# Longer transfers in the drain of a one-hot attention layer, and its last four blocks searched in wider segments

## The chip, the cores and the metric

The kernel runs on one core of a Trainium2 chip. The core has five engines, each with its own instruction queue: PE (matrix multiply; PEld is its weight load), DVE (vector), ACT (scalar functions), POOL (GpSimd) and SP (synchronisation; here it only issues transfers). Sixteen DMA engines move data between main memory and the on-chip memory. The metric is the device time of one execution in microseconds, as a median of several executions.

## The reference

`x` is 4096 x 512, `adj` is 4096 x 4096 (64 MB), `W` is 512 x 2048 (four heads), `a` is 4 x 1024 x 1, all in float32.

```python
ht = (h @ W).reshape(N, N_HEADS, N_HIDDEN).transpose(1, 0, 2)
src = jnp.einsum('hnd,hd->hn', ht, a_src)
dst = jnp.einsum('hnd,hd->hn', ht, a_dst)
e = jax.nn.leaky_relu(src[:, :, None] + dst[:, None, :], SLOPE) + adj_mat[None]
att = jax.nn.softmax(e, axis=-1)
h_prime = jnp.einsum('hij,hjd->hid', att, ht)
return h_prime.mean(axis=0)
...
x = _layernorm(x + _L0_gnn_ref(x, adj, L0_gnn_W, L0_gnn_a), axis=-1)
```

The nonzero entries of `adj` are random numbers up to 1e9 and are added to scores that are tiny beside them. So the softmax of a row is 1 at the largest entry of that row of `adj` and 0 elsewhere, as long as the largest leads the second by more than the scores can differ. Then the layer is: for each row find the column j of the largest entry, fetch `x[j]`, multiply it by the mean of the four heads' weights, add the row's own `x`, and normalise the row.

## The kernel before, in words

`leading_rows` does exactly that for all rows, and also proves on the chip that each row's largest entry leads by enough; a second function, `general`, does the full softmax and runs only if the proof fails for a row, which it does not on this data. The proof needs the two largest entries of each row, a bound from `W` and `a` (`head_norms`) and the largest norm of a row of `x` (`row_norm`, `bound`, `test`, `count`, `report`).

The 4096 rows are split into `NB` = 32 blocks of 128 rows, one row to a partition (row p * 32 + ib is partition p of block ib). For block `ib`:

- `load_adj` (L122, SP's queue) brings 128 rows of 16 KB of `adj`, 2 MB: whole for blocks 0 to 27, in halves for 28 to 30, in quarters for 31.
- `segment_maxima` (L169, DVE) takes the maximum of each segment of 16 columns (blocks 0 to 17, `E_EARLY`) or 32 columns (18 to 31, `E`): 256 or 128 maxima for a row.
- `find_segment` (L176, L178, DVE) finds the largest maxima of a row and the index of the first. Its index goes to POOL.
- `fetch_segment` (L185, L191, L198, POOL) turns the index into a row number (with `first`) and fetches that one segment of each row again from main memory with an indirect DMA into the tile `lead`; `start` is the segment's first column (with `width`).
- `find_column` (L208, L214, DVE; L216, L202, POOL) finds the column inside the segment and gathers the 128 rows `x[j]` into `y`. For block 31 `find_column_in_row` (L222) searches the whole row of 4096 on DVE instead, so that its gather waits for no segment.
- `turn` (PE transposes L229, ACT copy L231), `products` (PE, L244), `residual` (adds the row's own `x`, L237), `stats` (ACT), `rstd` (POOL) and `finish` (ACT, L277) end the block. The result overwrites the row's own `x` in the tile `hold` (32 x 512 numbers in each partition), and `store` (L329, SP's queue) writes it out.

Every engine runs its instructions in the order in which the program issues them. The loop over t = 0 to 31 runs the steps of different blocks in each turn: block t's maxima, block t - 2's column, block t - 3's products, block t - 6's end. `AHEAD` = 5 is how many blocks the loads run ahead.

**The drain.** `Q` = 4, `LATE` = 28, `BEHIND` = 24. `x` of blocks 24 to 27 is loaded last of all, after `adj` of block 31, at t = 31 (L441, two transfers of two blocks). Until it is there the products of 24 to 27 are kept in a spare buffer (`put_by`, L257), and `add_x` (L261) adds the `x`: on POOL for 24, 25 and 26, on DVE for 27. Stores of blocks 0 to 23 are issued only after the loop, behind every load on SP's queue: two of four blocks, then eight of two blocks (L482 to L485). After the loop POOL's order is: `add_x(24)` (L486), the column and the gather of block 30 (L487), the segment of block 31 (L488), `add_x(25)` (L489), the gather of block 31 (L490), `add_x(26)` (L491). DVE's order there is: the column of 30 (L214), the search of 31's row (L222), and later what ends blocks 28 to 31. The last stores (L540 to L542) go in this order: 28, 29, 24 with 25, 26 with 27, 30, 31.

Semaphores are placed by a framework: a transfer on SP's queue takes the next of eight completion semaphores in turn, and is not issued before the transfer eight places earlier has landed. Each of the 16 DMA engines raises the semaphore when its share has landed, and only all sixteen count as landed.

Of the kernel before, what the change touches and what calls it, by code (L numbers as in the profile page):

```python
# [9 lines left out]
F32 = mybir.dt.float32  # L10
U32 = mybir.dt.uint32
I32 = mybir.dt.int32
AF = mybir.ActivationFunctionType
OP = mybir.AluOpType
# [6 lines left out]
P = 128  # L21
C = 512
E = 32
E_EARLY = 16
EARLY = 18


@with_exitstack
# [40 lines left out]
def leading_rows(ctx, tc, x, adj, W, a, out, ident, v, n_bad, any_bad):  # L69
# [8 lines left out]
    nc = tc.nc  # L78
    N, D = x.shape
    H = a.shape[0]  # L80
    KB, NB, S = D // P, N // P, N // E
    S_EARLY = N // E_EARLY
    AHEAD = 5
    Q = 4
    PIECES = 4
    LATE = NB - Q
    BEHIND = LATE - Q

    once = ctx.enter_context(tc.tile_pool(name="once", bufs=1))
    adj_pool = ctx.enter_context(tc.tile_pool(name="adj_pool", bufs=AHEAD + 1))  # L90
    y_pool = ctx.enter_context(tc.tile_pool(name="y_pool", bufs=4))
    lead_pool = ctx.enter_context(tc.tile_pool(name="lead_pool", bufs=2 * Q + 1))
    small = ctx.enter_context(tc.tile_pool(name="small", bufs=5))
    rows = ctx.enter_context(tc.tile_pool(name="rows", bufs=2))
    psum = ctx.enter_context(tc.tile_pool(name="psum", bufs=4, space=bass.MemoryType.PSUM))

    adj_rows = adj.rearrange("(p nb) m -> nb p m", nb=NB)
    adj_segs = adj.rearrange("n (s e) -> (n s) e", e=E)
    adj_segs_early = adj.rearrange("n (s e) -> (n s) e", e=E_EARLY)
    x_rows = x.rearrange("(p nb) d -> p nb d", nb=NB)  # L100
    out_rows = out.rearrange("(p nb) d -> p nb d", nb=NB)
    w_blocks = W.rearrange("(kb p) (h d) -> p kb h d", p=P, h=H)
# [11 lines left out]
    def pieces(ib):  # L114
        return PIECES if ib == NB - 1 else 2 if ib >= LATE else 1

    def load_adj(ib):
        if 0 <= ib < NB:
            t = adj_t[ib] = adj_pool.tile([P, N], F32, name="adj_t")
            n = pieces(ib)  # L120
            for k in range(n):
                nc.sync.dma_start(t[:, ts(k, N // n)], adj_rows[ib][:, ts(k, N // n)])  # L122

    def load_x(lo, n):
        nc.sync.dma_start(hold[:, ds(lo, n), :], x_rows[:, ds(lo, n), :])
# [13 lines left out]

    make_identity(nc, ident)  # L140
    first = once.tile([P, NB], U32, name="first")
    nc.gpsimd.iota(first[:, :EARLY], pattern=[[S_EARLY, EARLY]], base=0, channel_multiplier=NB * S_EARLY)
    nc.gpsimd.iota(first[:, EARLY:], pattern=[[S, NB - EARLY]], base=EARLY * S, channel_multiplier=NB * S)
    ones = once.tile([P, P], F32, name="ones")
    nc.gpsimd.memset(ones, 1.0)
    width = once.tile([P, 2], U32, name="width")
    nc.gpsimd.iota(width, pattern=[[E_EARLY - E, 2]], base=E, channel_multiplier=0)
    power = once.tile([P, 3], F32, name="power")
    nc.gpsimd.memset(power, -0.5)
    eps = once.tile([P, 1], F32, name="eps")  # L150
# [6 lines left out]
    sd = once.tile([P, NB], F32, name="sd")  # L157
    lead_by = once.tile([P, 1], F32, name="lead_by")

    seg_of, at_of, lead_of, y_t, yt_of, o_ps = {}, {}, {}, {}, {}, {}  # L160

    def segment_maxima(ib, lo, hi):

        e = E_EARLY if ib < EARLY else E
        if lo == 0:
            seg_of[ib] = small.tile([P, N // e], F32, name=f"seg{e}", bufs=2)
        n = max(pieces(ib), 2)
        for k in range(lo * n // PIECES, hi * n // PIECES):
            nc.vector.tensor_reduce(  # L169
                seg_of[ib][:, ts(k, N // e // n)],  # L170
                adj_t[ib][:, ts(k, N // n)].rearrange("p (s e) -> p s e", e=e), axis=AX.X, op=OP.max,
            )
# [9 lines left out]
    def fetch_segment(ib):  # L182
        at = at_of.pop(ib)
        row = small.tile([P, 1], U32, name="row")
        nc.gpsimd.tensor_tensor(row, at[:, 0:1], first[:, ib : ib + 1], op=OP.add)  # L185
        early = ib < EARLY
        if early:
            lead = lead_pool.tile([P, E_EARLY], F32, name="lead_early", bufs=8)
        else:
            lead = lead_pool.tile([P, E], F32, name="lead")  # L190
        nc.gpsimd.indirect_dma_start(  # L191
            out=lead, out_offset=None, in_=adj_segs_early if early else adj_segs,
            in_offset=bass.IndirectOffsetOnAxis(ap=row[:, :1], axis=0),
        )
        lead_of[ib] = lead
        if ib < NB - 1:
            start = at_of[ib] = small.tile([P, 1], U32, name="start")
            nc.gpsimd.tensor_tensor(start, at[:, 0:1], width[:, int(early) : int(early) + 1], op=OP.mult)  # L198

    def gather_rows(ib, col):  # L200
        y = y_t[ib] = y_pool.tile([P, D], F32, name="y")
# [126 lines left out]
    def store(queue, lo, n):  # L328
        queue.dma_start(out_rows[:, ds(lo, n), :], hold[:, ds(lo, n), :])  # L329
# [93 lines left out]
    for t in range(NB):  # L423
        if t == NB // 2:
            tc.mark_branch_hint_location("general", engines=HINTED)
        if t in x_at:
            load_x(*x_at[t])
        if t + AHEAD == NB - 1:
            load_x(LATE, Q)
        load_adj(t + AHEAD)  # L430
        middle = 1 if t == NB - 1 else 2
        segment_maxima(t, 0, middle)
        if t >= COLUMN:
            find_column(t - COLUMN)
        segment_maxima(t, middle, PIECES)
        pair = FINISH <= t < BEHIND + FINISH and t % 2 == 0
        if pair:
            rstd(slice(t - FINISH, t - FINISH + 2))
        if t == NB - 1:
            for ib in (BEHIND, BEHIND + 2):  # L440
                load_x(ib, 2)  # L441
        find_segment(t)
        if t < 2:
            mean_of_heads(t)
        elif t == 2:
            mean_of_heads(2)
            mean_of_heads(3)
        if t == 0:
            turn_a()
        turned = [(*vectors[0], turn_w(*vectors.pop(0))) for _ in range(vectors_at.get(t, 0))]  # L450
        if t == 16:
            head_norms()
        ib = t - PROJECT
        if t == NB - 1:
            for late in range(LATE, NB):
                row_norm(late)
        if t == NB - 2:
            residual(LATE)
            residual(LATE + 1)
        if ib >= 0:  # L460
            turn(ib)
            if ib > BEHIND:
                products(ib - 1, KB - 1, KB)
            if ib < BEHIND:
                residual(ib)
        for some in turned:
            head_vector(*some)
        if ib >= 0:
            products(ib, 0, KB if ib < BEHIND else KB - 1)
        if t >= BEHIND + STATS:  # L470
            put_by(t - STATS)
        elif t >= STATS:
            stats(t - STATS)
            row_norm(t - STATS)
        if pair:
            finish(t - FINISH)
            finish(t - FINISH + 1)
# [1 line left out]
    for ib in range(BEHIND, LATE):  # L479
        row_norm(ib)  # L480
    nc.scalar.activation(xx, xx, AF.Sqrt)
    for ib in range(0, 2 * Q, Q):  # L482
        store(nc.sync, ib, Q)
    for ib in range(2 * Q, BEHIND, 2):
        store(nc.sync, ib, 2)  # L485
    add_x(nc.gpsimd, BEHIND)  # L486
    find_column(NB - 2)  # L487
    fetch_segment(NB - 1)  # L488
    add_x(nc.gpsimd, BEHIND + 1)  # L489
    find_column_in_row(NB - 1)  # L490
# [46 lines left out]
    moments(NB - 1)  # L537
    factor(NB - 1, shift=True)
    finish_in_halves(NB - 1)
    for ib, n in ((NB - 4, 1), (NB - 3, 1), (BEHIND, 2), (BEHIND + 2, 2), (NB - 2, 1)):  # L540
        store(nc.sync, ib, n)
    store(nc.sync, NB - 1, 1)  # L542

# [152 lines left out]
```

## Time and profile before

| What | us |
|---|---|
| median of three runs (235.43, 235.53, 236.70) | 235.53 |
| the profiled execution, its own time | 235.65 |
| its span, first to last instruction | 234.1 |
| around the span | 1.55 |
| DVE busy | 191.6 |
| PE busy | 197.5 |
| POOL busy | 100.3 |
| ACT busy | 111.6 |
| last quarter of `adj` of block 31 starts to be searched | 207.51 |
| gather of block 31 issued by POOL | 215.40 |
| first transpose of block 31 on PE | 222.62 |
| store of block 31 issued | 229.70 |

In the tables of the profile, L169 is line 169 of the kernel before. A row of the timeline has start, duration (both us), engine, line, operation, tile written and tiles read with their shapes, the number of instructions, and in brackets how long the engine was idle before and what ended that. A row of the windows has a stretch of time, its length, and for each engine the busy us in it; then the granted PE clock as a share, the mean busy share of the 16 DMA engines, and GB/s moved. In a row of waits stand the us waited in total, how often, and the longest.

Beside the tables the trace holds single DMA packets, with size and time, and the moment at which each of the 16 engines raised a transfer's semaphore. Where a size or a landing is given below without a table, it is from there.

### The profile page before, as it was taken

The numbers are of one execution on the slowest core, as the hardware profiler recorded it, in microseconds if no ns is written. First come the engines' busy times: TensorE is split into PE (matmuls) and PEld (weight loads), VectorE is DVE, ScalarE is ACT, GpSimd is POOL, SyncE is SP. The second block draws the span as 40 slices with busy tenths as digits, with TensorE's granted clock in tenths as the row PEclk, the third lists the DMA queues.
The fourth block names the chain that finished last, engine by engine and source line by source line (L and its number), as shares of the span: only waits on it lengthen the run. The fifth ranks groups of instructions, "written<-read, shape, count | busy, mean of one in ns | idle before, by whom it ended". The sixth has DMA issues, their size and how long they took to land.

```text
span 234.1 us, 2486 instructions
## 1 busy us (share of the span) xinstructions
PE 197.5 (84%) x683; PEld 101.6 (43%) x683; DVE 191.6 (82%) x300; ACT 111.6 (48%) x267; POOL 100.3 (43%) x212
## 2 busy tenths in 40 slices
PE   0198959999999699999999599859899967999980
PEld 0034525765656356555544144324333423344360
DVE  0566885589929999999789986999999999989871
ACT  2003012155665447475768264645564654187561
POOL 2022232415524464646443642646465464557400
PEclk9999778999999999999999979999999999999997
DMA  6999999999999999999999999999999999999994
GB/s 243 432 428 417 445 419 434 418 444 420 433 422 427 430 424 433 426 419 431 434 427 427 429 433 424 419 436 419 435 428 417 425 427 421 413 426 419 416 386 179
DMA packets 12977, 97.06 MB, mean 415 GB/s; under 512 B 2072, under 2 KB 2584, under 8 KB 7200
## 3 DMA queue, kind: packets, MB, share of 16 engines
q1 hardware_dynamic: 9360, 88.08, 89.0%
q0 software_dynamic: 3584, 8.77, 9.5%
q8 instruction: 6, 0.10, 0.2%
q14 instruction: 11, 0.09, 0.1%
q10 hardware_dynamic: 16, 0.02, 0.0%
HBM read 88.47 MB, written 8.39 MB: 414 GB/s over the span
## 4 chain that ended last, share of the span: by engine, by line
DMA 48%; POOL 19%; issue 17%; DVE 11%; PE 2%; ACT 0%; POOLq 0%; DVEq 0%; ACTq 0%; SPq 0%
DMA adj_t<-in_adj_dram 41%; DVE seg L169 8%; POOL y L202 6%; POOL lead L191 5%; DMA y<-in_x_dram,col 3%; DMA lead<-in_adj_dram,row 2%; POOL sd L272 2%; PE o L286 2%; DMA a_rows<-in_L_gnn_a_dram 1%; DVE col L222 1%; POOL row L185 1%; POOL start L198 1%; POOL col L216 1%; POOL lead_early L191 1%; DVE at L178 1%
## 5 line engine op out<-in xcount | busy, mean ns | idle before, releaser
L169 DVE TENSOR_REDUCE seg<-adj_t 128x128 f32<-128x2048 f32 (+2 forms) x66 | 145.4, 2207 | 29.0 <-DMA adj_t<-in_adj_dram 29.0
L244 PE MATMUL o<-w_sum,yt 128*128 128x512 f32 x248 | 116.0, 609 | 0.7 <-ACT yt L231 0.7
L244 PEld LDWEIGHTS o<-w_sum,yt 128*128 128x128 f32 x248 | 44.8, 193 | 53.9 <-issue 42.4
L231 ACT COPY yt<-tp 128x512 f32<-128x512 f32 x32 | 18.8, 587 | 45.8 <-PE tp L229 45.7
L202 POOL DMA_INDIRECT y<-in_x_dram,col x32 | 30.8, 961 | 16.5 <-POOL col L216 15.4
L334 PE MATMUL o<-hold,ident 128*128 128x512 f32 x32 | 20.9, 815 | 14.6 <-DMA hold<-in_L_gnn_W_dram 14.6
L229 PE MATMUL tp<-ident,y 128*128 128x128 f32 x128 | 19.7, 276 | 13.7 <-DMA y<-in_x_dram,col 13.7
L237 PE MATMUL o<-hold,ident 128*128 128x512 f32 x52 | 26.8, 600 | 0.0
L229 PEld LDWEIGHTS tp<-ident,y 128*128 128x128 f32 x128 | 14.4, 141 | 26.8 <-issue 25.5
L185 POOL TENSOR_TENSOR row<-at,first 128x1 uint32<-128x1 uint32 x32 | 6.0, 188 | 43.7 <-DVE at L178 43.3
L352 ACT COPY wt<-tp 128x512 f32<-128x512 f32 x16 | 9.2, 586 | 31.5 <-PE tp L350 31.5
L191 POOL DMA_INDIRECT lead_early<-in_adj_dram,row x18 | 18.1, 1008 | 8.9 <-POOL row L185 8.9
L216 POOL TENSOR_TENSOR col<-start,within 128x1 uint32<-128x1 uint32 x31 | 5.8, 188 | 36.0 <-DVE within L214 36.0
L251 ACT ACTIVATE sq<-hold 128x512 f32<-128x512 f32 x32 | 19.8, 619 | 0.0
L358 PEld LDWEIGHTS pv<-at_d,wt 128*128 128x128 f32 x128 | 16.3, 191 | 6.8 <-ACT wt L352 3.7
L334 PEld LDWEIGHTS o<-hold,ident 128*128 128x128 f32 x32 | 8.1, 265 | 25.1 <-issue 20.2
L335 ACT ACTIVATE w_sum<-o 128x512 f32<-128x512 f32 x4 | 2.4, 598 | 33.0 <-PE o L334 33.0
L277 ACT ACTIVATE hold<-o,nm,sd 128x512 f32<-128x512 f32 x24 | 17.2, 769 | 0.0
L191 POOL DMA_INDIRECT lead<-in_adj_dram,row x14 | 14.0, 1003 | 7.0 <-POOL row L185 7.0
L268 ACT ACTIVATE sq<-o,nm 128x512 f32<-128x512 f32 x24 | 16.5, 687 | 0.8
L358 PE MATMUL pv<-at_d,wt 128*128 128x2 f32 x128 | 15.3, 244 | 0.6 <-ACT wt L352 0.6
L266 ACT ACTIVATE sq<-o 128x512 f32<-128x512 f32 x24 | 14.6, 609 | 0.0
(91 smaller groups left out, 150.8 us busy)
## 6 DMA issues: line engine op xcount, KB each, us to landing
adj_t<-in_adj_dram SPq DMA_DIRECT2D x28, 2048.0 KB, 31.7
adj_t<-in_adj_dram SPq DMA_DIRECT2D x6, 1024.0 KB, 28.0
out_dram<-hold SPq DMA_DIRECT2D x10, 512.0 KB, 14.3
hold<-in_L_gnn_W_dram SPq DMA_DIRECT2D x4, 1024.0 KB, 18.8
hold<-in_x_dram SPq DMA_DIRECT2D x2, 2048.0 KB, 36.5
hold<-in_x_dram SPq DMA_DIRECT2D x3, 1024.0 KB, 27.8
adj_t<-in_adj_dram SPq DMA_DIRECT2D x4, 512.0 KB, 19.7
out_dram<-hold SPq DMA_DIRECT2D x2, 1024.0 KB, 13.8
```

Source lines behind the costliest of these rows:

```text
L169: nc.vector.tensor_reduce(seg_of[ib][:, ts(k, N // e // n)], adj_t[ib][:, ts(k, N // n)].rearrange("p (s e) -> p s e", e=e), axis=AX.X, op ...
L191: nc.gpsimd.indirect_dma_start(out=lead, out_offset=None, in_=adj_segs_early if early else adj_segs, in_offset=bass.IndirectOffsetOnAxis(a ...
L202: nc.gpsimd.indirect_dma_start(out=y, out_offset=None, in_=x, in_offset=bass.IndirectOffsetOnAxis(ap=col[:, :1], axis=0),)
L229: nc.tensor.transpose(tp[:, kb, :], y[:, ts(kb, P)], ident)
L231: nc.scalar.copy(yt, tp)
L237: nc.tensor.matmul(o_ps[ib], ident, hold[:, ib, :], start=start, stop=False)
L244: nc.tensor.matmul(o_ps[ib], yt_of[ib][:, kb, :], w_sum[:, kb, :], start=(start and kb == 0), stop=(kb == KB - 1),)
L251: nc.scalar.activation(sq, hold[:, ib, :], AF.Square, accum_out=xx[:, ib : ib + 1])
L268: nc.scalar.activation(sq, o, AF.Square, bias=nm[:, i], accum_out=sd[:, i])
L277: nc.scalar.activation(hold[:, ib, :], o_ps.pop(ib), AF.Identity, bias=nm[:, i], scale=sd[:, i])
L334: nc.tensor.matmul(o, ident, hold[:, w_at + kb * H + h, :], start=(h == 0), stop=(h == H - 1))
L358: nc.tensor.matmul(pv[:, kb, h : 2 * H : H], wt[:, k, :], at_d[:, k, h : 2 * H : H], start=(k == 0), stop=(k == KB - 1),)
```

## The change

Five things change, all in `leading_rows`:

- `x` of blocks 24 to 27 is loaded with one transfer of 1 MB instead of two of 512 KB.
- Results of blocks 8 to 23 are stored with four transfers of four blocks instead of eight of two blocks.
- Results of blocks 28 and 29 are stored with one transfer of two blocks instead of two of one block.
- Blocks 28 to 31 are searched in 64 segments of 64 columns instead of 128 segments of 32; the segment fetched again is then 256 B for a row.
- The bookkeeping for the widths becomes a table (`spans`) with three entries: `first` and `width` are filled by three small instructions each on POOL at the start (two and one before), and the `lead` tiles have 8, 8 and 4 buffers (8 and 9 before, of two widths).

```diff
+E_LAST = 64
 EARLY = 18
+LAST = 4
...
-    lead_pool = ctx.enter_context(tc.tile_pool(name="lead_pool", bufs=2 * Q + 1))
+    lead_pool = ctx.enter_context(tc.tile_pool(name="lead_pool", bufs=1))
+    LEADS = (8, 8, LAST)
...
-    adj_segs = adj.rearrange("n (s e) -> (n s) e", e=E)
-    adj_segs_early = adj.rearrange("n (s e) -> (n s) e", e=E_EARLY)
+    spans = ((E_EARLY, 0, EARLY), (E, EARLY, NB - LAST), (E_LAST, NB - LAST, NB))
+    adj_segs = {e: adj.rearrange("n (s e) -> (n s) e", e=e) for e, _, _ in spans}
...
-    nc.gpsimd.iota(first[:, :EARLY], pattern=[[S_EARLY, EARLY]], base=0, channel_multiplier=NB * S_EARLY)
-    nc.gpsimd.iota(first[:, EARLY:], pattern=[[S, NB - EARLY]], base=EARLY * S, channel_multiplier=NB * S)
+    for e, lo, hi in spans:
+        nc.gpsimd.iota(
+            first[:, lo:hi], pattern=[[N // e, hi - lo]], base=lo * N // e, channel_multiplier=NB * N // e
+        )
...
-    width = once.tile([P, 2], U32, name="width")
-    nc.gpsimd.iota(width, pattern=[[E_EARLY - E, 2]], base=E, channel_multiplier=0)
+    width = once.tile([P, len(spans)], U32, name="width")
+    for k, (e, _, _) in enumerate(spans):
+        nc.gpsimd.iota(width[:, k : k + 1], pattern=[[0, 1]], base=e, channel_multiplier=0)
...
+    def span_of(ib):
+        return next(k for k, (_, lo, hi) in enumerate(spans) if lo <= ib < hi)
...
-        e = E_EARLY if ib < EARLY else E
+        e = spans[span_of(ib)][0]
...
-        early = ib < EARLY
-        if early:
-            lead = lead_pool.tile([P, E_EARLY], F32, name="lead_early", bufs=8)
-        else:
-            lead = lead_pool.tile([P, E], F32, name="lead")
+        k = span_of(ib)
+        e = spans[k][0]
+        lead = lead_pool.tile([P, e], F32, name=f"lead{e}", bufs=LEADS[k])
         nc.gpsimd.indirect_dma_start(
-            out=lead, out_offset=None, in_=adj_segs_early if early else adj_segs,
+            out=lead, out_offset=None, in_=adj_segs[e],
             in_offset=bass.IndirectOffsetOnAxis(ap=row[:, :1], axis=0),
         )
...
-            nc.gpsimd.tensor_tensor(start, at[:, 0:1], width[:, int(early) : int(early) + 1], op=OP.mult)
+            nc.gpsimd.tensor_tensor(start, at[:, 0:1], width[:, k : k + 1], op=OP.mult)
...
         if t == NB - 1:
-            for ib in (BEHIND, BEHIND + 2):
-                load_x(ib, 2)
+            load_x(BEHIND, Q)
...
-    for ib in range(0, 2 * Q, Q):
+    for ib in range(0, BEHIND, Q):
         store(nc.sync, ib, Q)
-    for ib in range(2 * Q, BEHIND, 2):
-        store(nc.sync, ib, 2)
...
-    for ib, n in ((NB - 4, 1), (NB - 3, 1), (BEHIND, 2), (BEHIND + 2, 2), (NB - 2, 1)):
+    for ib, n in ((LATE, 2), (BEHIND, 2), (BEHIND + 2, 2), (NB - 2, 1)):
         store(nc.sync, ib, n)
     store(nc.sync, NB - 1, 1)
```

More of the change, by code (lines that the diff above doesn't have):

```diff
@@ L80, in leading_rows @@
     H = a.shape[0]
-    KB, NB, S = D // P, N // P, N // E
-    S_EARLY = N // E_EARLY
+    KB, NB = D // P, N // P
     AHEAD = 5
```

## The prediction

> **What bounds the kernel now.** I read the page first: DMA and its rate stay level to the end, so until the last slice the bytes set the pace.
>
> ```profile
> DMA  6999999999999999999999999999999999999994
> GB/s 243 432 428 417 445 419 434 418 444 420 433 422 427 430 424 433 426 419 431 434 427 427 429 433 424 419 436 419 435 428 417 425 427 421 413 426 419 416 386 179
> ```
>
> Nothing before 186 us changes, so I then read the drain alone, by the windows: stretch, length, busy us of PE, PEld, DVE, ACT, POOL, granted clock, DMA share, GB/s.
>
> ```profile
> 208.00:212.00 4.00, 4.00 (x12) 1.72 (x11) 3.52 (x8) 3.62 (x12) 2.42 (x4) 1.00 1.03 430
> 216.00:220.00 4.00, 3.82 (x15) 1.68 (x15) 3.39 (x22) 3.11 (x8) 1.64 (x2) 1.00 1.03 417
> 224.00:228.00 4.00, 3.64 (x17) 2.88 (x16) 3.17 (x9) 3.07 (x6) 0.00 (x0) 1.00 0.93 367
> 228.00:230.00 2.00, 0.00 (x0) 0.00 (x0) 1.10 (x5) 0.86 (x2) 0.00 (x0) 1.00 0.98 394
> 230.00:232.00 2.00, 0.00 (x0) 0.00 (x0) 0.00 (x0) 0.00 (x0) 0.00 (x0) 0.89 0.47 180
> ```
>
> The DMA is full until 230; the engines are done at about 229.7. So two things end together: the queue of stores, and the chain of block 31. The chain from 204 us (start, us, what):
>
> ```profile
> 204.23 5.55 DMA lead<-in_adj_dram,row
> ...
> 210.14 3.29 DVE col L222 x2
> ...
> 213.44 1.28 POOL adj_t L261
> ...
> 215.40 7.09 DMA y<-in_x_dram,col
> ...
> 222.62 0.63 PE tp L229 x4
> ...
> 229.11 0.56 ACT hold L326
> ```
>
> The segment of block 30 lets DVE search block 31's row; POOL's addition of x of block 25 is the last work ahead of the gather; the gather lands and 7.1 us later the last store is issued (229.70). POOL's timeline shows what stands ahead of it:
>
> ```profile
> 208.75 1.27 POOL L261 TENSOR_TENSOR adj_t<-adj_t,hold 128x512 f32<-128x512 f32 x1 [1.86 <-ACT sq L251]
> 210.22 0.19 POOL L216 TENSOR_TENSOR col<-start,within 128x1 uint32<-128x1 uint32 x1 [0.20 <-DVE within L214]
> 211.01 0.97 POOL L202 DMA_INDIRECT y<-in_x_dram,col  x1 [0.60 <-POOL col L216]
> 212.46 0.96 POOL L191 DMA_INDIRECT lead<-in_adj_dram,row  x1 [0.27 <-POOL row L185]
> 213.44 1.28 POOL L261 TENSOR_TENSOR adj_t<-adj_t,hold 128x512 f32<-128x512 f32 x1
> ```
>
> The 1.86 us ahead of the first row end 0.21 us after x of 24 and 25 landed (208.54); x of 26 and 27 landed at 209.85. ACT, named there, was done at 208.17.
>
> Which of the two ends the run is seen in the semaphores: fifteen engines raise that of the last store at 231.53 to 231.86 (1.83 to 2.16 us after its issue), one at 232.84. That one is about a microsecond behind from block 14's store on (222.68; next slowest 221.34) and works without a pause: 230.04 (24 and 25), 231.29 (26 and 27), 231.97 (30), 232.84. The end follows it by 1.2 us. So the backlog of the slowest engine ends the run, and the chain has up to 232.84 - 231.86 = 0.98 us to spare.
>
> **The change, part by part.**
>
> *Packet times.* A row of 8192 B takes 309 ns on its engine, one of 4096 B 159, one of 2048 B 84. Each engine carries 8 of the 128 rows. x of 24 to 27: 16 x 159 becomes 8 x 309, -0.072 us. Blocks 8 to 23: 64 x 159 becomes 32 x 309, -0.288. Blocks 28 and 29: 16 x 84 becomes 8 x 159, -0.072. Six transfers fewer (one load, four stores, one store), six semaphore packets of 9 ns: -0.054. The four `lead` fetches have one packet on each engine, 46 ns for 1024 B, now 2048 B (84): +0.152. Sum **-0.33 us** on each engine, with the path as long as the slowest engine stays busy. The bounds: 0 if the straggler is set by something else, -0.49 if the wider segments cost nothing.
>
> The Trainium skill, "DMA: Bandwidth & Descriptors", section Anatomy of one DMA, gives each DMA a fixed 2.0 us plus its bytes. By it six transfers fewer would be worth 6 x 2.0 = 12 us if each paid alone. The windows show the engines 93 to 103% busy over these transfers, so that cost lies under the next transfer's data, and the trace decides.
>
> *Issue on SP.* Six issues fewer, 0.33 us each, on a queue that mostly waits for the transfer eight places back. The stores of 4 to 23 go out earlier, but behind the same bytes. Block 28 waits for 29 (normalised at 222.10), while the slowest engine reaches them only at 227.6. Nothing, since the queue covers it; if that engine ran dry, one 256 KB store, 0.67 us, would be late.
>
> *Wider segments on DVE.* The reduction reads the same 2048 columns: 2272 ns to 128 maxima, 2271 to 64, so nothing. The maxima search took 428 ns on 256 and 295 on 128: on 64 about 228; the index search 419 and 285: about 218. A block saves 0.134 us. Inside the segment 16 columns take 169 and 32 take 185; I take +0.03 on 64. Block 30's segment is thus asked for 3 x 0.134 - 0.03 = 0.37 us earlier and lands at 209.42; block 31's own search still waits for its last quarter (207.51). Block 31's row search then ends at 214.63 - 0.34 = 214.29. The search for the second largest (L208, four of eight wider, +0.13) delays the proof's test, done at 218.96 + 0.18; PE's count, which waits for it, then comes at 220.2 anyway (below). Four more POOL set-up instructions (3 + 3 for 2 + 1, near 0.15 us each) lie in the first 15 us.
>
> *The added wait on POOL.* `add_x(24)` now waits for all four blocks of x: 209.85 - 0.07 + 0.21 = 209.99 instead of 208.75. Queued behind it are block 30's column and gather, block 31's segment, `add_x(25)` and block 31's gather. Addition 1.27, to 211.26; column to 211.49. From there to a gather it is 0.60 where POOL waited for DVE first, 0.26 where the instruction was ready (block 31's segment after its row). Here it is ready, so 211.75, and 212.09 at the other bound. To the end of `add_x(25)` it was 3.71 (211.01 to 214.72): 215.46 to 215.80. Block 31's gather needs the search's end plus 0.72 (215.01) and follows the addition by 0.03 to 0.68: **215.5 to 216.5**; I take 215.5, since its index is then 1.2 us old. So POOL takes back what DVE won.
>
> *The gathers beside longer rows.* A gather beside 8 KB rows landed 6.6, 6.7 and 6.9 us after its issue (185.28, 190.62, 205.93), beside 4 KB rows 6.1, 6.2 and 7.1 (201.28, 211.01, 215.40). The 7.1 ends on the straggling engine, the other fifteen had it by 221.75, 6.35 after the issue. So +0.5 us beside long rows (bounds: -0.5 and +0.85). The same page, section Queues, rings and completion order, speaks against the change here: an engine alternates between queues after whole packets. Four gather packets an engine behind four rows of 150 ns more would make +0.6; the trace's gathers say 0.5, and they decide.
>
> *From there to the end.* Block 30's gather goes out at 211.75 and lands 6.64 later, at 218.4 instead of 217.17. PE turns it at 218.5 (217.50 before), then needs 0.66 + 1.02 + 0.16 + 2.84 = 4.68 us to block 31's turn: 223.2. Block 31 itself lands at 222.1 to 223.1. So the turn moves from 222.62 to 223.2, the last store from 229.70 to 230.26: **+0.56 on the chain**, not yet on the end, for 0.98 were spare. Fifteen engines then land at 232.1 to 232.4, the slowest, its backlog 0.33 shorter, at 232.5.
>
> *Sum.* The end follows the slowest engine: 234.1 - 0.33. The profiled execution, 235.65, becomes 235.3; it lay 0.12 over the median of 235.53, so the median becomes **235.2**.
>
> **The rivals.**
>
> *The wait on x decides (slower).* If POOL recovers nothing, block 31's gather is at 216.45, and with +0.5 beside long rows the turn is 1.55 late. That exceeds the spare 0.98: 232.84 + 0.57, time 236.1; with the upper bound of the gather, +0.85, 1.9 late, 236.5. It decides from a last store issued after 230.68. For it: POOL's order, every step queued. Against it: 0.26 for a ready instruction, and DVE's earlier end.
>
> *The straggler goes (faster).* If its lateness falls elsewhere, the chain alone sets the end. With the gather where it was, the last store lands at 231.86: -0.98, time 234.55; with DVE's 0.34 kept as well, 234.2. For it: the lag appears at one place, near 220 us, where the trace shows an 8 KB instruction load on one engine. Against it: nothing in the change removes that load, and POOL's wait spends the gain.
>
> *Nothing happens.* The packets are saved, the straggler falls 0.3 us further back with the longer rows (one 8 KB row): 235.5.
>
> **How the numbers follow.** 0.5% (1.18 us) is about what a measurement of this kernel can tell from no change. Forecast 0.45 (own range 234.8 to 235.5, from -0.49 with a little of the chain, to 0); wait decides 0.27, with a longer stretch of the gathers behind it; straggler goes 0.17; nothing 0.11. Range 234.2 to 236.6: it takes in the ends of both outer cases. Faster by over 0.5% (under 234.35) needs the third case near its end with a shorter gather too: 0.18. Slower (over 236.7) needs the wait and a landing beyond the rows seen: 0.22. The rest, 0.60, is within.
>
> **What would show it.** Right: `add_x(24)` starts near 210.0, the gather of block 31 near 215.5, its turn near 223.2, the last store near 230.3; one engine's semaphores still a microsecond behind; stores of 8 to 23 with 309 ns a row. Wrong: a last store after 230.7 with the end behind it by 4.4 or less (the wait decides), or all sixteen engines landing it together (the straggler went).

## The result and the profile after

The changed kernel takes 236.29 us (median) against 235.56 us: ratio 1.0033, 95% interval 1.0020 to 1.0045. That is a small loss, inside the 0.5% that was named as the limit and inside the range, but on the other side of "no change" from the forecast of 235.2. The profiled execution took 236.43 us; its span is 234.9 us.

POOL does what the prediction said, to a tenth of a microsecond. Its timeline in the changed kernel (start, duration, engine, line, operation, tiles, idle before); L267 is the addition of x, L208 a gather, L197 a segment fetch:

```profile
210.04 1.27 POOL L267 TENSOR_TENSOR adj_t<-adj_t,hold 128x512 f32<-128x512 f32 x1 [3.40 <-ACT adj_t L263]
211.74 0.97 POOL L208 DMA_INDIRECT y<-in_x_dram,col  x1 [0.27 <-POOL col L222]
213.19 0.96 POOL L197 DMA_INDIRECT lead<-in_adj_dram,row  x1 [0.27 <-POOL row L193]
215.60 0.96 POOL L208 DMA_INDIRECT y<-in_x_dram,col  x1 [0.16 <-issue]
```

The first addition waits 3.40 us where it waited 1.86 us, and starts at 210.04 (predicted 209.99); block 30's gather goes out at 211.74 (211.75), block 31's at 215.60 (215.5). The row to look at is the third: the segment of block 31 is asked for at 213.19 instead of 212.46. The chain of the changed kernel goes through just that fetch, which was in no step of the chain before:

```profile
209.79 3.40 DVE col L228 x2
213.19 6.60 DMA lead<-in_adj_dram,row
219.79 0.02 issue
219.81 0.23 DVE inner L214
...
221.07 0.19 DVE gap L411
221.26 0.04 issue
221.31 0.22 PE px L415 x2
221.53 2.77 PE o L250 x6
224.30 0.44 PE tp L235 x4
```

Block 31's segment lands at 219.79. Only then can DVE find the second largest entry inside it (L214) and run the proof's test (L405 to L411); PE's count (L415) waits for the test, block 30's products (L250) stand behind the count on PE, and block 31's turn (L235) behind the products. DVE's eight second-largest searches run in one go in the kernel before (first row); in the changed kernel the eighth, that of block 31, waits for its segment, and DVE's waits show this as a new row (second row):

```profile
216.87 1.06 DVE L208 MAX8 inner<-lead 128x8 f32<-128x32 f32 x8
```

```profile
DVE inner L214 <- DMA lead<-in_adj_dram,row: 1.8, 1, 1.8
```

PE's timeline, before and then after, shows what it does to PE. The first row is block 30's turn, then block 29's last product, the count, three products of block 30, block 31's turn:

```profile
217.50 0.66 PE L229 MATMUL tp<-ident,y 128*128 128x128 f32 x4
217.99 1.02 PE L244 MATMUL o<-w_sum,yt 128*128 128x512 f32 x2
219.20 0.22 PE L409 MATMUL px<-gap,ones 128*1 128x32 f32 x2 [0.18 <-DVE gap L405]
219.35 2.84 PE L244 MATMUL o<-w_sum,yt 128*128 128x512 f32 x6
222.62 0.63 PE L229 MATMUL tp<-ident,y 128*128 128x128 f32 x4 [0.43 <-DMA y<-in_x_dram,col]
```

```profile
219.22 0.63 PE L235 MATMUL tp<-ident,y 128*128 128x128 f32 x4 [1.31 <-DMA y<-in_x_dram,col]
219.69 1.02 PE L250 MATMUL o<-w_sum,yt 128*128 128x512 f32 x2
221.31 0.22 PE L415 MATMUL px<-gap,ones 128*1 128x32 f32 x2 [0.60 <-DVE gap L411]
221.46 2.84 PE L250 MATMUL o<-w_sum,yt 128*128 128x512 f32 x6
224.14 0.60 PE L235 MATMUL tp<-ident,y 128*128 128x128 f32 x4
```

In the kernel before, the count was also held by DVE, for 0.18 us, and the end of that row names it: the test stood on PE's path already, with next to nothing to spare. After, PE waits 1.31 us for block 30's gather and 0.60 us for the test, and block 31's turn waits for PE, not for its own gather (landed 223.21). The turn is 1.52 us later, the last store goes out at 231.20 instead of 229.70 (+1.50).

The stores ahead of it move by as much: that of blocks 24 and 25 goes out at 226.80 instead of 225.31. So the end changes its owner. The windows (stretch, length, busy us of PE, PEld, DVE, ACT, POOL, granted clock, DMA share, GB/s) show the DMA engines running out of work ahead of it, where they were full before:

```profile
224.00:228.00 4.00, 4.00 (x19) 2.93 (x18) 3.82 (x11) 3.23 (x7) 0.00 (x0) 1.00 0.71 287
228.00:230.00 2.00, 1.13 (x6) 0.65 (x4) 1.24 (x4) 0.67 (x2) 0.00 (x0) 1.00 0.75 301
```

From 224 to 228 the share is 0.71 (0.93 before). Fifteen engines raise the last store's semaphore at 233.01 to 233.49 (231.53 to 231.86 before): they had run dry and waited for the store to be issued. The sixteenth raises it at 233.74, and it is not the engine that trailed before. That one is still a microsecond late with blocks 28 and 29 (228.70, next slowest 227.65), but has caught up by the store of 24 and 25 (229.91). Packets that follow one another without a gap show the new last one: it carries a 16 KB instruction load from 227.43 to 229.21 and then works without a pause to the end. In the kernel before such a load, 0.97 us from 225.89 on, fell on an engine that had time to spare. So the late stores put the landing at 233.49 on fifteen engines, and the one with this load is 0.25 us later in this trace.

### The profile page after: what moved, and what is told of

Its sections match the earlier page's. It is cut to its first block, busy times and chain, and to the rows that moved or that the text cites. A ratio compares the mean times of both kernels' runs of the same rounds, so it can differ in the third digit from the quotient of the medians.

```text
span 234.9 us, 2475 instructions
## 1 busy us (share of the span) xinstructions
PE 196.3 (84%) x683; PEld 101.3 (43%) x683; DVE 191.3 (81%) x300; ACT 111.9 (48%) x267; POOL 100.5 (43%) x215
## 4 chain that ended last, share of the span: by engine, by line
DMA 47%; POOL 18%; issue 17%; DVE 12%; PE 3%; ACT 0%; POOLq 0%; DVEq 0%; ACTq 0%; SPq 0%
DMA adj_t<-in_adj_dram 40%; DVE seg L177 8%; POOL lead L197 6%; POOL y L208 6%; DMA lead<-in_adj_dram,row 5%; POOL sd L278 2%; PE o L250 2%; PE o L292 2%; DMA a_rows<-in_L_gnn_a_dram 1%; DVE col L228 1%; POOL row L193 1%; POOL start L204 1%; POOL col L222 1%; DVE at L186 1%; DVE top L184 1%
## 5 line engine op out<-in xcount | busy, mean ns | idle before, releaser
L177 DVE TENSOR_REDUCE seg<-adj_t 128x128 f32<-128x2048 f32 (+3 forms) x66 | 145.4, 2207 | 28.9 <-DMA adj_t<-in_adj_dram 28.8
L250 PE MATMUL o<-w_sum,yt 128*128 128x512 f32 x248 | 114.6, 603 | 0.7 <-ACT yt L237 0.7
L250 PEld LDWEIGHTS o<-w_sum,yt 128*128 128x128 f32 x248 | 44.4, 191 | 53.4 <-issue 42.0
L197 POOL DMA_INDIRECT lead<-in_adj_dram,row x32 | 32.2, 1006 | 15.1 <-POOL row L193 15.1
L208 POOL DMA_INDIRECT y<-in_x_dram,col x32 | 30.8, 961 | 16.2 <-POOL col L222 16.1
L235 PE MATMUL tp<-ident,y 128*128 128x128 f32 x128 | 20.1, 280 | 16.6 <-DMA y<-in_x_dram,col 16.6
L340 PE MATMUL o<-hold,ident 128*128 128x512 f32 x32 | 19.7, 774 | 14.4 <-DMA hold<-in_L_gnn_W_dram 14.4
L243 PE MATMUL o<-hold,ident 128*128 128x512 f32 x52 | 27.5, 615 | 0.0
L235 PEld LDWEIGHTS tp<-ident,y 128*128 128x128 f32 x128 | 14.7, 143 | 29.7 <-issue 28.3
L340 PEld LDWEIGHTS o<-hold,ident 128*128 128x128 f32 x32 | 7.6, 250 | 24.2 <-issue 19.5
L184 DVE MAX8 top<-seg 128x8 f32<-128x256 f32 (+2 forms) x32 | 11.6, 361 | 1.1
```

The costliest lines, as they stand in the source:

```text
L177: nc.vector.tensor_reduce(seg_of[ib][:, ts(k, N // e // n)], adj_t[ib][:, ts(k, N // n)].rearrange("p (s e) -> p s e", e=e), axis=AX.X, op ...
L197: nc.gpsimd.indirect_dma_start(out=lead, out_offset=None, in_=adj_segs[e], in_offset=bass.IndirectOffsetOnAxis(ap=row[:, :1], axis=0),)
L208: nc.gpsimd.indirect_dma_start(out=y, out_offset=None, in_=x, in_offset=bass.IndirectOffsetOnAxis(ap=col[:, :1], axis=0),)
L235: nc.tensor.transpose(tp[:, kb, :], y[:, ts(kb, P)], ident)
L243: nc.tensor.matmul(o_ps[ib], ident, hold[:, ib, :], start=start, stop=False)
L250: nc.tensor.matmul(o_ps[ib], yt_of[ib][:, kb, :], w_sum[:, kb, :], start=(start and kb == 0), stop=(kb == KB - 1),)
```

## The experiments

The theory formed from these traces, called the theory of the proof: the one transfer of x delays block 31's segment fetch on POOL, the longer rows of the stores delay its landing, and both together push DVE's test and PE's count past the cover that the slowest DMA engine gave. Rivals: the wait for x alone, the long rows alone, the wider segments, the late gathers. Each run below was timed beside the kernel before, whose median was 235.54 to 235.57 in every group.

**x in two transfers again**

```diff
-            load_x(BEHIND, Q)
+            for ib in (BEHIND, BEHIND + 2):
+                load_x(ib, 2)
```

> The changed kernel with x of blocks 24 to 27 loaded in two transfers again; all else as changed. Theory of the proof (the wait for x on POOL puts block 31's segment fetch late, its landing holds DVE's inner maximum, the test and PE's count, and block 30's products stand behind the count): the first addition of x starts near 208.8 again instead of 210.04, block 31's segment is fetched near 212.2 (213.19 in the changed kernel) and lands near 218.7, the count runs near 220.3 (221.31), block 31's turn near 223.3 (224.30); time 235.3 to 235.7. Rival, long rows: only the longer stores slow the gathers, the wait for x costs nothing: count near 221.2, time 236.2.

Measured: 235.25 us, ratio 0.9987 (0.9978 to 0.9996): faster than both kernels. First addition 208.93, segment asked for at 212.07 and landed at 218.30, count 219.81, turn 222.68, last store 229.76. The wait for x is needed for the loss; that the long rows alone carry it falls.

**Stores of 8 to 23 in twos again**

```diff
-    for ib in range(0, BEHIND, Q):
+    for ib in range(0, 2 * Q, Q):
         store(nc.sync, ib, Q)
+    for ib in range(2 * Q, BEHIND, 2):
+        store(nc.sync, ib, 2)
```

> The changed kernel with results of blocks 8 to 23 stored in eight transfers of two blocks again; all else as changed. Theory of the proof: block 31's segment is still fetched near 213.2, but lands beside 4 KB rows after 5.3 to 5.7 us instead of 6.6, near 218.7; count near 220.2; turn of block 31 near 223.2; time 235.4 to 235.8. Rival, wait for x alone: the landing stays near 219.8 and the time near 236.3. Rival, long rows alone: all of the loss is gone, the landing at or before 217.8 and the time at 235.3 or less.

Measured: 235.79 us, ratio 1.0011 (1.0002 to 1.0020). The segment is asked for at 213.16, as in the changed kernel, and lands after 5.87 us instead of 6.60, at 219.03; count 220.55, turn 223.38, last store 230.44. So the long rows are needed for most of the loss: with short rows beside the same wait for x, 0.5 us of 0.73 is gone.

**Only the wider segments**

Of the changed kernel, all three edits to transfers are taken back:

```diff
-            load_x(BEHIND, Q)
+            for ib in (BEHIND, BEHIND + 2):
+                load_x(ib, 2)
...
-    for ib in range(0, BEHIND, Q):
+    for ib in range(0, 2 * Q, Q):
         store(nc.sync, ib, Q)
+    for ib in range(2 * Q, BEHIND, 2):
+        store(nc.sync, ib, 2)
...
-    for ib, n in ((LATE, 2), (BEHIND, 2), (BEHIND + 2, 2), (NB - 2, 1)):
+    for ib, n in ((NB - 4, 1), (NB - 3, 1), (BEHIND, 2), (BEHIND + 2, 2), (NB - 2, 1)):
```

> The kernel before with only the wider segments for blocks 28 to 31 (transfers as before). Theory of the proof: DVE starts block 31's row search near 209.8 instead of 210.14, POOL's steps behind it are 0.3 earlier, block 31's segment lands near 217.4 (217.71 before), the count near 218.9 (219.19); the end is held by the slowest DMA engine's stores and moves by at most the 0.15 us of larger segments: 235.4 to 235.7. Rival, the wider segments themselves cost (256 B for a row land later, or the wider inner search is on the path): the landing at 218.2 or later, time 235.9 or more.

Measured: 235.69 us, ratio 1.0004 (0.9995 to 1.0013). DVE and POOL are earlier as expected: the segment of block 31 lands at 217.18, the count runs at 218.70, and the last store goes out at 228.79, 0.91 us earlier than before. The slowest engine still lands it at 232.87 (232.84 before). This is the plainest sight of the cover: the chain won 0.9 us and the end did not move, because one engine's stores were not done.

**The whole proof behind block 31's products**

```diff
-    for ib in range(BEHIND, NB):
+    for ib in range(BEHIND, NB - 1):
         find_inner(ib)
     bound(3)
-    test()
...
-    pg = count()
     products(NB - 2, 0, KB - 1)
-    report(pg)
...
     moments(LATE - 1)
+    find_inner(NB - 1)
+    test()
...
     products_of_half(NB - 1, 1)
+    pg = count()
...
     finish_in_halves(NB - 1)
+    report(pg)
```

> The changed kernel with the proof taken off PE's path: block 31's inner maximum and the test follow the moments of block 27 on DVE, the count follows block 31's products on PE, the report comes last on DVE. Theory of the proof: block 30's products no longer stand behind the count, so PE turns block 31 as soon as its gather lands (223.2 to 223.5 instead of 224.30); the last store goes out near 230.3 instead of 231.20; time 235.3 to 235.7. Rival, the gather of block 31 alone sets the turn: the turn stays at 224.2 or later and the time at 236.2.

Measured: 241.53 us, ratio 1.0261 (1.0247 to 1.0275), against every expectation. The turn came at 223.80, at its own gather (landed 223.67), and the last store was down at 232.88, earlier than in the changed kernel. But the flag of the proof, which every engine reads before the kernel ends, was there only at 231.1. After reading it POOL needs 1.48 us and then 5.31 us to drain its queue of indirect transfers. Those two are in every trace here; in the kernel before POOL reads the flag at 221.5 and is done at 229.93, under the last stores; here it is done only at 239.42. So this run says nothing against the theory, but it isn't clean evidence for it either, and two smaller moves were tried.

**Only x in one transfer**

```diff
-            for ib in (BEHIND, BEHIND + 2):
-                load_x(ib, 2)
+            load_x(BEHIND, Q)
```

> The kernel before with only x of blocks 24 to 27 loaded in one transfer. Theory of the proof: the first addition starts near 210.0 (208.75 before), block 31's segment is fetched near 213.2, and beside 4 KB rows lands 5.3 to 5.9 later, near 218.7; count near 220.2 (219.19), turn of block 31 near 223.2 (222.62), last store near 230.3; since the slowest DMA engine's stores give the end up to 0.98 us of cover, the time moves little: 235.4 to 235.9. Rival, long rows alone: no later landing, no change in the last store (229.7). Rival, the wait for x alone: time 236.2.

Measured: 235.65 us, ratio 1.0006 (0.9998 to 1.0015): no loss that shows, as expected. Its one profile is of an execution of 236.48 in which DVE's search of block 31's row ended at 216.34 (214.63 before), so its steps on POOL are not read here. That delay is older than the drain: the segment of block 12 is asked for at 103.19 (98.60 before) and that of block 30 still 1.67 us late.

**Only the longer stores of 8 to 23**

```diff
-    for ib in range(0, 2 * Q, Q):
+    for ib in range(0, BEHIND, Q):
         store(nc.sync, ib, Q)
-    for ib in range(2 * Q, BEHIND, 2):
-        store(nc.sync, ib, 2)
```

> The kernel before with only the results of blocks 8 to 23 stored in four transfers of four blocks. Theory of the proof: POOL keeps its times, but the gathers land beside 8 KB rows: block 30's 0.3 to 1.2 later than 217.17, block 31's segment 0.5 to 1.3 later than 217.71; count 219.7 to 220.5; last store 229.9 to 230.6; the slowest engine's stores end 0.3 earlier; time 235.1 to 235.5. Rival, long rows alone carry the loss: time 236.0 or more.

Measured: median 235.18 us, ratio 1.0001 (0.9982 to 1.0021). Block 30's gather lands at 217.74 (217.17 before), the segment at 218.26 (217.71), count 219.75, last store 230.05, and the slowest engine lands it at 232.77. The interval is wide because four of twelve executions took 236.3 to 236.9 and eight 235.0 to 235.3; no trace of this kernel is of the first kind, so that spread stays open.

**POOL's first addition behind the two fetches**

```diff
-    add_x(nc.gpsimd, BEHIND)
     find_column(NB - 2)
     fetch_segment(NB - 1)
+    add_x(nc.gpsimd, BEHIND)
     add_x(nc.gpsimd, BEHIND + 1)
```

> The changed kernel with POOL's first addition of x moved behind the gather of block 30 and the segment fetch of block 31, so that neither stands behind the one transfer of x. Theory of the proof: block 30's gather goes out near 210.5 (211.74 in the changed kernel), block 31's segment near 212.0 (213.19) and lands near 218.4; block 31's gather stays near 215.5 behind two additions; count near 220.0, turn of block 31 near 223.3 and held by its own gather (223.2); last store near 230.3; time 235.3 to 235.6. Rival, long rows: the landing stays near 219.8 and the time near 236.2.

Measured: 235.44 us, ratio 0.9997 (0.9982 to 1.0012), with x in one transfer and the long stores kept. Block 30's gather goes out at 210.88, the segment at 212.33, landing at 218.67; count 220.19; turn 223.76, held by block 31's own gather (issued 215.97, landed 223.63). Taking two fetches out from behind one wait gives back the loss in the median; two of twelve executions took 236.4 and 236.8.

**Only the count behind three products**

```diff
-    pg = count()
     products(NB - 2, 0, KB - 1)
-    report(pg)
+    pg = count()
...
     moments(LATE - 1)
+    report(pg)
```

> The changed kernel with only PE's count moved behind three of block 30's four products, and the report of the proof behind the moments of block 27 on DVE. Theory of the proof: the products start when block 30's copy is there (220.5) and not after the count (221.31), so block 31 is turned near 223.4, when its gather lands, instead of 224.14; last store near 230.5 instead of 231.20; time 235.5 to 235.9. Rival, the late turn has another cause (block 30's own late gather, or block 31's): the turn stays at 224.0 or later, time 236.2.

Measured: 236.93 us, ratio 1.0047 (1.0030 to 1.0064): a miss. The turn came at 225.00. PE was idle for 1.84 us ahead of block 30's turn, and the granted clock (the third number from the right) then fell to a half:

```profile
219.00:220.00 1.00, 0.81 (x4) 0.84 (x5) 0.21 (x2) 0.00 (x0) 0.00 (x0) 0.58 1.05 442
220.00:221.00 1.00, 1.00 (x4) 0.46 (x3) 0.93 (x8) 0.69 (x2) 0.00 (x0) 0.50 0.90 373
221.00:222.00 1.00, 1.00 (x3) 0.48 (x2) 0.20 (x2) 0.97 (x3) 0.00 (x0) 0.50 1.09 446
222.00:223.00 1.00, 1.00 (x2) 0.30 (x2) 0.88 (x2) 0.40 (x3) 0.46 (x2) 0.71 1.00 418
```

```profile
219.19 1.09 PE L235 MATMUL tp<-ident,y 128*128 128x128 f32 x4 [1.84 <-DMA y<-in_x_dram,col]
220.07 4.85 PE L250 MATMUL o<-w_sum,yt 128*128 128x512 f32 x8
```

The four transposes take 1.09 us instead of 0.63, and four products 4.85 us where the kernel before needs 1.02 + 2.84. The half clock lasts 3.4 us, 219.2 to 222.6. The Trainium skill, "TensorE: Matmul & The Clock Gate", Part 1, describes such a gate, with a free-running window of about 3.4 us; the length agrees. The same page's table "Why this matters for your kernels" advises to avoid idle gaps over about 3 us, which would not have warned of a gap of 1.84 us. The later count makes the flag late here too: POOL's queue is drained only at 234.54, level with the last landing at 234.42, so this order had little to spare on that side either.

**The wait for block 31's segment taken away**

```diff
-        nc.vector.max(out=inner[:, ib, :], in_=lead_of[ib])
+        nc.vector.max(out=inner[:, ib, :], in_=top[:, ib, :] if ib == NB - 1 else lead_of[ib])
```

> The changed kernel, but for block 31 the second-largest entry inside the leading segment is not searched: its place is filled from the eight largest segment maxima, so the proof of block 31 is incomplete and waits for no fetch (the fetch itself stays). This takes away only the wait of DVE for block 31's segment. Theory of the proof: the count on PE comes right after block 30's turn and the product of 29, near 220.2 instead of 221.31; the products of block 30 start near 220.5; block 31 is turned near 223.4, as its gather lands, instead of 224.14; last store near 230.4 instead of 231.20; time 235.4 to 235.7 against 236.3. Rival, the late gathers of blocks 30 and 31 alone hold the turn: it stays near 224.1 and the time at 236.2. A half clock on PE after its wait for block 30's gather would show in the granted clock and cost 1 to 2 us.

Measured: median 235.50 us, 0.79 us under the changed kernel (0.55 under its second measurement, below); against the kernel before the ratio is 1.0009 (0.9992 to 1.0026). The fetch is issued and lands as before the edit (213.12, 219.44), block 30's and 31's gathers land as late as in the changed kernel (218.87, 223.13), but nothing waits for the segment. PE:

```profile
219.01 0.63 PE L235 MATMUL tp<-ident,y 128*128 128x128 f32 x4 [1.61 <-DMA y<-in_x_dram,col]
219.47 1.02 PE L250 MATMUL o<-w_sum,yt 128*128 128x512 f32 x2
220.43 0.22 PE L415 MATMUL px<-gap,ones 128*1 128x32 f32 x2
220.58 2.84 PE L250 MATMUL o<-w_sum,yt 128*128 128x512 f32 x6
223.27 0.63 PE L235 MATMUL tp<-ident,y 128*128 128x128 f32 x4
```

The count follows the product at once, the turn is at 223.27 and the last store at 230.35, where the forecast had 223.2 and 230.26. This is the cleanest test of the theory: one wait away, all late gathers kept, and the turn is 0.87 us and the last store 0.85 us earlier. The time is less clean. Nine of twelve executions took 235.1 to 235.7, but three took 236.9 and none of those was traced; whether PE's clock fell in them after the gap of 1.61 us, as in the run above, is not shown. Beside the next kernel, which was timed in the same group with the changed kernel's chain, the median gains 0.35 us.

**Segments of 32 columns with all the long transfers**

```diff
-E_LAST = 64
+E_LAST = 32
...
-        lead = lead_pool.tile([P, e], F32, name=f"lead{e}", bufs=LEADS[k])
+        lead = lead_pool.tile([P, e], F32, name=f"lead{k}", bufs=LEADS[k])
```

> The changed kernel with blocks 28 to 31 searched in segments of 32 columns again; all transfers as changed. Theory of the proof: POOL is held by x (first addition near 210.0) whatever DVE does, so block 31's segment is still fetched near 213.2 and lands near 219.6; count near 221.1; time 236.0 to 236.4. Rival, the wider segments cost: landing at 219.0 or earlier and time 235.8 or less.

Measured: 235.85 us, ratio 1.0007 (0.9998 to 1.0016), with the same times on the chain as the changed kernel: segment asked for at 213.09, landed at 219.79, count 221.27, last store 231.16. Trace and time did not fit together, so both kernels were run side by side on one chip.

> The changed kernel, unaltered, beside the one with 32 columns on the same chip. Theory of the proof (wider segments cost nothing): both medians within 0.2 us of each other, near 236.0 to 236.3. Rival (wider segments cost): the changed kernel 0.3 to 0.5 us above the other, 236.2 to 236.4 against 235.8 to 235.9.

> The changed kernel with blocks 28 to 31 in segments of 32 columns, beside the changed kernel on the same chip. Theory of the proof: within 0.2 us of the changed kernel; block 31's segment lands within 0.2 us of its landing there. Rival (wider segments cost): 0.3 to 0.5 us below it, and the landing earlier by as much.

Measured side by side: 236.05 us with 64 columns, 235.96 with 32. The wider segments cost nothing that can be told. The 0.4 us between the earlier medians came from different groups of runs and did not return side by side, so differences of 0.2 to 0.4 us between groups should not be read; the loss of the change itself is 0.5 to 0.7 us (the second ratio of the changed kernel is 1.0023, 1.0012 to 1.0033).

**Only the longer stores, of 8 to 23 and of 28 with 29**

```diff
-    for ib, n in ((NB - 4, 1), (NB - 3, 1), (BEHIND, 2), (BEHIND + 2, 2), (NB - 2, 1)):
+    for ib, n in ((LATE, 2), (BEHIND, 2), (BEHIND + 2, 2), (NB - 2, 1)):
```

(with the edit to the stores of 8 to 23 shown above, in the kernel before)

> The kernel before with the longer stores of 8 to 23 and of 28 with 29, and nothing else. Theory of the proof: POOL keeps its times (first addition near 208.8, segment of block 31 near 212.4), the segment lands near 218.5 beside long rows, count near 219.8, last store near 230.0, inside the cover of the slowest engine's stores, which end 0.4 earlier: 235.1 to 235.4. Rival, long rows: 236.0 or more.

Measured: median 235.22 us, ratio 0.9994 (0.9979 to 1.0008). First addition 208.73, segment landed 218.46, count 219.94, last store 230.07, landed at 232.60 (232.84 before). The packet saving shows in the landing once the chain leaves it room; in the time the interval takes in no change, since three of twelve executions took 236.0 to 236.5.

**x in two transfers, and POOL's fetches first**

```diff
-    add_x(nc.gpsimd, BEHIND)
     find_column(NB - 2)
     fetch_segment(NB - 1)
-    add_x(nc.gpsimd, BEHIND + 1)
+    add_x(nc.gpsimd, BEHIND)
     find_column_in_row(NB - 1)
+    add_x(nc.gpsimd, BEHIND + 1)
     add_x(nc.gpsimd, BEHIND + 2)
```

(with the edit to x shown first, in the changed kernel)

> The changed kernel with x loaded in two transfers again, and POOL's order changed so that the gather of block 30 and the segment of block 31 come ahead of the first addition and the gather of block 31 ahead of the second. A try for a version that beats both. Theory of the proof: block 30's gather near 210.5, block 31's segment near 211.9, block 31's gather near 214.7; count near 219.7; last store near 229.6; then the slowest engine's stores end the run as with x in two: 235.1 to 235.4. Rival, a late second addition holds ACT's statistics and block 30's copy: last store after 230.0, time 235.6 or more.

Measured: 235.34 us, ratio 0.9983 (0.9972 to 0.9993). Last store 229.56, landed 232.76. It beats the kernel before as well, and is no better than x in two transfers alone (235.25): the last store is 0.2 us earlier and the slowest engine's stores are not.

The runs in one table: when the last store is issued, when the last of the sixteen engines has it, and the median.

| Kernel | last store issued | landed | us |
|---|---|---|---|
| wider segments only | 228.79 | 232.87 | 235.69 |
| x in two, POOL's order | 229.56 | 232.76 | 235.34 |
| before | 229.70 | 232.84 | 235.56 |
| x in two | 229.76 | 232.58 | 235.25 |
| longer stores only (8 to 23, 28 and 29) | 230.07 | 232.60 | 235.22 |
| no wait for block 31's segment | 230.35 | 232.61 | 235.50 |
| short stores | 230.44 | 232.96 | 235.79 |
| first addition behind | 230.84 | 233.06 | 235.44 |
| 32 columns | 231.16 | 233.43 | 235.85 |
| changed | 231.20 | 233.74 | 236.29 |

Up to about 230.4 the landing does not follow the store: it stays at 232.6 to 233.0, the end of the slowest engine's backlog. Beyond, it follows. In every row the store of 24 and 25 goes out 4.4 us ahead of the last, so a late chain moves all the last stores together. This is why the parts do not add: the wait for x alone (+0.1 by the median) and the long stores alone (-0.4 by the median, an interval that takes in 0) are each within the cover or a gain, and together they step over it.

## Why the prediction was wrong, step by step

- **What bounds the kernel: right.** Chain and slowest DMA engine end together, with about 0.98 us of cover for the chain. The run with only the wider segments shows it directly.
- **Packet times: right in sign, too large in size.** Where the chain stays inside the cover the last landing is 0.24 to 0.26 us earlier (longer stores, x in two; one trace each). By the prediction's rows the longer stores alone should have given 0.288 + 0.072 + 5 x 0.009 = 0.40. It took the recorded durations, but on a busy engine the next row starts 4 ns before the recorded end of the last: eight rows of 4096 B take 1.243 us (before, from 229.697) and eight of 8192 B 2.447 us (x in two, from 224.514), so a merged pair saves 5 ns and not 9, which makes 0.22. No run shows the 12 us that it quoted and set aside; the section quoted describes transfers issued from GpSimd, and these are SP's.
- **Issue on SP: right in that it cost nothing by itself.** Blocks 28 and 29 went out at 224.24, 2.1 us later than block 29 before, because its normalisation was late; the run with only the longer stores shows no cost of the merger.
- **Wider segments on DVE: right on the durations** (the search on 64 maxima took 0.23 and 0.22 us, the one in the segment 0.22 and not 0.215) and on the row search (214.29 forecast and measured; 213.81 in the second trace of the same kernel, so the match to 0.01 us is chance).
- **The added wait on POOL: right** to 0.1 us at each step, the 0.27 us of a ready instruction included. The rival that priced POOL's wait as unrecovered (gather at 216.45, time 236.1) had the right sign and nearly the right time, by a path that did not occur: the wait for x did decide, but through block 31's segment and not through its gather, which went out at 215.60.
- **The sentence that failed** is the one on the second-largest search: it "delays the proof's test, done at 218.96 + 0.18; PE's count, which waits for it, then comes at 220.2 anyway". It costed the search by its own length (+0.13) and not by what it waits for. The prediction had itself moved block 31's segment fetch (it names it as queued behind the addition) and did not follow it to its reader. In the kernel before that fetch landed at 217.71 and the last search ended at 217.93, so there was no slack between the two. The fetch went out 0.73 us later and took 6.60 us instead of 5.25: landing +2.08, count 221.31 instead of 220.2, turn 224.14 instead of 223.2, last store 231.20 instead of 230.26. With the wait taken away the forecast's own numbers came out within 0.1 us (223.27, 230.35), but partly by luck: block 30's turn came 0.5 us later than forecast (219.01 for 218.5), and PE's stretch from there to block 31's turn took 4.26 us and not 4.68, since the sum 0.66 + 1.02 + 0.16 + 2.84 adds durations that overlap.
- **The gathers beside longer rows: mis-sized.** +0.5 us was taken, with 0.85 as the upper bound. Block 31's gather took 7.61 (7.09 before, +0.5), but block 30's 7.35 (6.16, +1.2) and the segment behind it in the same queue +1.35. Across the runs block 30's gather took 6.16, 6.26 and 6.60 us beside short stores (before, wider segments only, short stores) and 6.84 to 7.48 beside long ones. The rows that the prediction went by also left out the gather issued at 195.95, which took 7.53 us, mostly beside 4 KB rows: the spread at one row length was as large as the difference that was read from them. Why the delay is up to 1.2 us, twice what alternating with rows of 150 ns more would make, is not explained by these runs.

## What to carry to other kernels

When a transfer is merged, list every instruction that is queued behind its waiter, and follow each of them to its reader, the bookkeeping ones (a proof, a count) as well: an instruction that ends exactly when its reader wants it is on the path, even if the chain of waits does not name it. Two steps that are each harmless may share one cover; add their delays before asking whether it hides them. Merge the stores that nobody waits for, and keep in pieces the load whose first half has a reader: that kernel (x in two transfers) beats both, the kernel before by 0.3 us.

## What the runs showed of the hardware

- After its last branch POOL, which issued the indirect transfers, spends 1.48 + 5.31 us in every trace here; from reading the flag to the end of this it took 8.4 us before (221.54 to 229.93) and 8.3 us with the late proof (231.11 to 239.42). It is hidden as long as POOL reads the flag some 8 us ahead of the last landing (an estimate from these two); with the flag at 231.1 it put the end at 240.3.
- In one trace PE's granted clock fell to 0.5 for 3.4 us after a gap of 1.84 us in which it had waited for one late gather; a gap of 1.31 or 1.61 us at the same place (changed kernel, no wait for the segment) did not do it in the traces taken.
- One of the sixteen DMA engines lands its stores 0.8 to 1.3 us behind the next slowest from about 221 us to the end in the traces of before and of the wider segments alone, and sets when a full queue ends. In the changed kernel's trace another one is last from the store of 24 and 25 on: it carries the 16 KB instruction load of 1.78 us at 227.43, and lands up to 1.4 us behind the next slowest.
